# A two-layer convolution block on one core: the first statistics shared between two engines, parked products issued between them, two banks for the first running sums

## The chip, the core and the metric

The kernel runs on one core of a Trainium2 chip. The core has five engines that matter here, each with its own in-order list of instructions: PE (TensorE, matrix products), DVE (VectorE), ACT (ScalarE), POOL (GpSimd) and SP (SyncE, which here only issues DMAs). The metric is the device time of one execution in microseconds (us), as a median over runs.

## What is computed

The input x has 384 channels of 192x192 float32. Two layers follow each other; only the first matters for this change. Its shape, cut to the core:

```python
def _gn(v, G=32, eps=1e-5):                     # normalise over groups of 12 channels
    g = v.reshape(B_, G, C_ // G, H_, W_)
    m, s = jnp.mean(g, axis=(2, 3, 4)), jnp.var(g, axis=(2, 3, 4))
    return ((g - m) / jnp.sqrt(s + eps)).reshape(v.shape)

def layer0(x):                                  # x already normalised
    qkv = einsum('bchw,oc->bohw', x, w_qkv)     # 384 -> 1152 channels
    qkv = max over 2x2 pixels, then 3x3 depthwise convolution
    ...                                         # channel attention with top-k, gelu, projection

x = x + layer0(_gn(x))
x = x + conv7x7_depthwise(_gn(x))
```

Before any product of the first layer can be right, the mean and the variance of every group of 12 channels over all 36,864 pixels must be known, so all of x (56.6 MB) is read once for statistics alone.

## The kernel before

The 384 channels lie on three tiles of 128 partitions (`KT` = 3; the first two are `TWO`). The pixels are cut into 24 blocks (`NB`) of 8 image rows, 1536 pixels each (`BLK`). Statistics run over the blocks from 23 down to 0. The last three of them (2, 1, 0: `NX` = 3) stay in SBUF in the tiles `held`, because the products begin with them.

**First two tiles (lines 392 to 434).** SP loads one block of both tiles at a time (`xs`, 1536 KB) into a pool `xsp` of five buffers; a buffer can be loaded again when the engine that measured it is done. `summed` (335) measures a block on DVE, three `bn_stats` of 512 pixels for each tile. After block 3, `aggregate` (353) joins what has been measured into a mean and a variance per channel; three small products on PE (`total`, 339) make the group means `mids`, and `moments` (359) expresses the channel's moments about such a mean. The channels of the last group that tile two shares with tile three are measured apart (`xe`, 317). After block 0, `both` (367) adds the last three blocks, and `normed` (373) gives `rstd0`, with a power on POOL (382). ACT scales the rows of the weights `wq` of these two tiles by it (434).

**Parked products (436 to 470).** `begin(i)` multiplies one third of a held block by the weights of the first two channel tiles, and ACT copies the partial sum from its PSUM bank into SBUF (`spots`); the products of the third tile are added later. There are 24 such products. Twenty are copied away and the last four stay in their banks. Four banks (`bank_b0`, `bank_b1`, `bank_c`, `bank_d`) are used in turn, so a product needs the copy of the one four places before it. 21 of the products are issued in one loop (453) before the third tile's statistics, and three more after that tile's `most`.

**Third tile (457 to 482).** The same statistics for the third tile. From block 22 down to 4 two blocks are loaded at once (`xt`, 128x3072, six `bn_stats`), then block 3, then the held ones. After block 3 the group mean is made on PE (463), and at the end `both`, `total` and `normed` give the third tile's scale. Its weights are scaled on ACT (506), and `pooled` (665) adds the third tile's products (678) to the parked sums.

**After that (1014 to 1090).** In the loop over the blocks 0 and 1, DVE takes the 2x2 maximum (688) and runs the 3x3 depthwise sums of block 0 (`depthwise`, 719): nine steps for each of six channel tiles, the running sum in a PSUM bank. `sum_bank` (788) gives the bank: while block 0 is summed, the next of `bank_x`, `bank_y`, `bank_r` in turn. A finished sum is transposed by DVE (833) and squared by ACT (746). Then a loop over groups begins with `share`, `base` and `second` (1051 to 1066), whose products go to `bank_x` and `bank_y` and are copied by ACT (1055, 1061).

The order on an engine is what the framework's scheduler makes of the program; calls wrapped in `keep` stay in program order. The DMA queue of SP is in program order.

Of the kernel before, what the change touches and what calls it, by code (L numbers as in the profile page):

```python
# [8 lines left out]
F32 = mybir.dt.float32  # L9
AF = mybir.ActivationFunctionType  # L10
ALU = mybir.AluOpType
AX = mybir.AxisListType

P = 128
C = 384
KT = C // P
# [3 lines left out]
PS = HW // 2  # L20
# [6 lines left out]
NB = PS // PR  # L27
IR = 2 * PR
BLK = IR * HW
PB = PR * PS  # L30
SUB = BLK // 512
NX = 3
# [54 lines left out]
def conv_preact_d2(  # L87
# [17 lines left out]
    nc = tc.nc  # L105
# [153 lines left out]
    def load_x(b, name):  # L259
# [14 lines left out]
    bank_x, bank_y, bank_b0, bank_b1, bank_c, bank_d = [  # L274
        pb.tile([P, 512], F32, name=f"bank_{n}") for n in ("x", "y", "b0", "b1", "c", "d")
    ]
    pr = qx.enter_context(tc.tile_pool(name="pr", bufs=1, space=PSUM))
    bank_r = pr.tile([P, 512], F32, name="bank_r")

    def turns_of(banks):  # L280

        k = -1
        while True:
            k += 1
            yield banks[k % len(banks)]

    small = turns_of([bank_x, bank_y, bank_r])
# [10 lines left out]
    spots = [rowbuf[:, k * 512 : (k + 1) * 512] for k in range(3 * KT * ROW // 512)]  # L298
# [7 lines left out]
    TWO = KT - 1  # L306
    OVER = TWO * P // GC * GC + GC - TWO * P
    keep = tc.keep_in_program_order
    with tc.tile_pool(name="stp", bufs=1) as stp, tc.tile_pool(name="xsp", bufs=5) as xsp:
        st = stp.tile([P, KT, NB * SUB, 6], F32, name="st0")  # L310
# [21 lines left out]
        none = stp.tile([P, CT], F32, name="none")  # L332
        nc.gpsimd.memset(none, 0.0)

        def summed(kt, b, n, t):
            for j in range(n * SUB):
                nc.vector.bn_stats(st[:, kt, b * SUB + j, :], t[:, j * 512 : (j + 1) * 512])

        def total(name, n, terms):

# [9 lines left out]
        def sel(kt, jt):  # L350
            return gsel[:, kt, jt * P : (jt + 1) * P]

        def aggregate(kt, lo, hi, name):

            mv = stp.tile([P, 2], F32, name=f"mv0_{kt}_{name}")
            nc.vector.bn_aggr(mv, st[:, kt, lo * SUB : hi * SUB, :].rearrange("p n s -> p (n s)"))
            return mv

        def moments(mv, mid, name):

            d = stp.tile([P, 2], F32, name=f"ds0_{name}")
            nc.vector.tensor_tensor(d[:, 0:1], mv[:, 0:1], mid, ALU.subtract)
            nc.vector.tensor_tensor(d[:, 1:2], d[:, 0:1], d[:, 0:1], ALU.mult)
            nc.vector.tensor_tensor(d[:, 1:2], d[:, 1:2], mv[:, 1:2], ALU.add)
            return d

        def both(kt, most, mid):

            last = moments(aggregate(kt, 0, NX, "last"), mid, f"{kt}_last")
            nc.vector.scalar_tensor_tensor(most, last, NX / NB, most, ALU.mult, ALU.add)  # L370
            return most

# [14 lines left out]
        mids = stp.tile([P, KT + 1], F32, name="mids0")  # L387
        mve = stp.tile([P, 2], F32, name="mve")
        me = stp.tile([P, 1], F32, name="me")
        rest0 = (NB - NX) / NB  # L390
        most = [None] * KT
        for b in reversed(range(NB)):
            if b == NX - 1:
                most[:TWO] = [aggregate(kt, NX, NB, "most") for kt in range(TWO)]
                means = [mv[:, 0:1] for mv in most[:TWO]]
                terms = [
                    [(sel(0, 0), means[0]), (sel(1, 0), means[1])],
                    [(sel(0, 1), means[0]), (sel(1, 1), means[1]), (shared[:, 0:P], me)],
                    [(of, means[1]), (ones, me)],
                ]  # L400
                for k, i in ((0, 0), (1, 1), (KT, 2)):
                    ps = total(f"gs_mid0_{k}", 1, terms[i])
                    nc.vector.tensor_scalar_mul(mids[:, k : k + 1], ps, 1.0 / GC)
                de = moments(mve, mids[:, KT : KT + 1], "e")
                nc.vector.tensor_scalar_mul(de, de, 1.0 / EP)
                dm = [moments(most[kt], mids[:, kt : kt + 1], f"{kt}_most") for kt in range(TWO)]
                for d in dm:
                    nc.vector.tensor_scalar_mul(d, d, rest0)
            if b < NX:
                xb = held[b][:, 0:TWO]  # L410
            else:
                xb = xsp.tile([P, TWO, BLK], F32, name=f"xs{b}", tag="xs")
            nc.sync.dma_start(xb, xv[:, 0:TWO, b * BLK : (b + 1) * BLK])
            for kt in range(TWO):
                summed(kt, b, 1, xb[:, kt])
            if b == NB - 1:
                for j in range(EN // 384):
                    nc.vector.bn_stats(ste[:, j, :], xe[:, j * 384 : (j + 1) * 384])
                nc.vector.bn_aggr(mve, ste.rearrange("p n s -> p (n s)"))
                nc.vector.tensor_scalar_mul(me, mve[:, 0:1], 1.0 / EP)  # L420
        ds = [both(kt, dm[kt], mids[:, kt : kt + 1]) for kt in range(TWO)]
        terms = [
            [(sel(0, 0), ds[0]), (sel(1, 0), ds[1])],
# [12 lines left out]
        def begin(i):  # L436
            b, ct, g = begun_qk[i]
            ps = next(large)
            rows = held[b].rearrange("p t (r c) -> p t r c", c=HW)
            for kt in range(TWO):  # L440
                keep(
                    nc.tensor.matmul(
                        ps, wq[:, kt, ct * P : (ct + 1) * P], rows[:, kt, :, g * 64 : (g + 1) * 64],
                        start=(kt == 0), stop=(kt == TWO - 1), skip_group_check=True,
                    )
                )
            if i < len(spots):
                nc.scalar.copy(spots[i], ps)
                sums_qk[b, ct, g] = spots[i], False
            else:  # L450
                sums_qk[b, ct, g] = ps, True

        for i in range(len(spots) + 1):
            begin(i)


        kt = TWO
        mid = mids[:, kt : kt + 1]
        for b in [*range(NB - 2, NX, -2), NX, *reversed(range(NX))]:
            n = 2 if b > NX else 1  # L460
            if b == NX - 1:
                most = aggregate(kt, NX, NB, "most")
                ps = total(
                    "gs_mid0_2", 1,
                    [(sel(1, 2), means[1]), (shared[:, P:], me), (whole, most[:, 0:1])],
                )
                nc.vector.tensor_scalar_mul(mid, ps, 1.0 / GC)
                dm = moments(most, mid, "2_most")
                nc.vector.tensor_scalar_mul(dm, dm, rest0)
                for i in range(len(spots) + 1, len(begun_qk)):  # L470
                    begin(i)
            if b < NX:
                xb = held[b][:, kt]
            else:
                xb = xsp.tile([P, TWO, BLK], F32, name=f"xt{b}", tag="xs")
                xb = xb.rearrange("p k n -> p (k n)")[:, 0 : n * BLK]
            loaded = nc.sync.dma_start(xb, xv[:, kt, b * BLK : (b + n) * BLK]).ins
            summed(kt, b, n, xb)
        d = both(kt, dm, mid)
# [97 lines left out]
    with ExitStack() as bx:  # L577
# [141 lines left out]
        def depthwise(b, ct, dst, pin):  # L719

            r0 = b % 3 * PR
            acc = sum_bank(b)[:, 0:C].rearrange("p (r c) -> p r c", c=PS)
            for tap in range(9):
                i, j = divmod(tap, 3)
                src = ring[ct][:, r0 + i : r0 + i + PR, j : j + PS]
                w = wd[:, ct, tap : tap + 1]
                if tap == 0:
                    pin(
                        nc.vector.tensor_scalar(
                            acc, src, w, bdb[:, ct : ct + 1], ALU.mult, ALU.add  # L730
                        )
                    )
                else:
                    into = dst if tap == 8 else acc
                    pin(nc.vector.scalar_tensor_tensor(into, src, w, acc, ALU.mult, ALU.add))
                yield
# [48 lines left out]
        turning = {}  # L785
        sides = {}

        def sum_bank(b):

            if sum_pool is not None:  # L790
                return sum_pool.tile([P, C], F32, name=f"acc{b}", tag="tr")
            return next(small) if b == 0 else bank_r

        def pe_keep(ins):
            return keep(ins) if ins.ins.engine == mybir.EngineType.PE else ins
# [218 lines left out]
        last = None  # L1014
        for b in range(2):
            xb = held.pop(b)
            for ct in range(2 * KT):
# [13 lines left out]
                if last is not None:  # L1031
                    finish(*last)
                    last = None
                if b > 0:
                    last = b - 1, ct, dst, taps
# [55 lines left out]
        for n, (b, pair, half) in enumerate(groups):  # L1091
            s = n % 6
# [36 lines left out]
            if s in (4, 5) or (s == 0 and b > 2):  # L1129
                bb, p = (b, s - 4) if s else (b - 1, KT - 1)  # L1130
# [5 lines left out]
            first = early if scaling else early + 1 + (s < 4)  # L1136
# [249 lines left out]
    with tc.tile_pool(name="ap", bufs=1) as ap:  # L1386
# [8 lines left out]
        i = AHEAD - 1  # L1395
# [28 lines left out]
    for i in range(3):  # L1424
        t = sxp.tile([P, LEAD + CP * RB * RUN + LEAD], F32, name=f"sx{i}")
# [137 lines left out]
    for i in range(AHEAD, NBC):  # L1563
        j = i - 2
# [61 lines left out]
    with ExitStack() as ex_:  # L1626
# [255 lines left out]
        last = None  # L1882

        later = {2 * kt: kt for kt in range(1, KT)}
        for n in range(steps):
# [8 lines left out]
            apart = outp.tile([P, CP, 2, NT * NJ], F32, name=f"apart{n}", tag="apart", bufs=3)  # L1894
# [24 lines left out]
            for q in range(CP):  # L1919
                ps = sums(q, range(2 if q in ahead else 0, 3))  # L1920
                c = n * CB + 2 * q
# [24 lines left out]
            last = apart  # L1946
# [58 lines left out]
```

## Time and profile before

| | us |
|---|---|
| runs | 2703.38, 2695.53, 2695.43 |
| median | 2695.53 |
| profiled execution | 2711.91 |
| its span, first to last instruction | 2710.2 |

| engine | busy in the span, us |
|---|---|
| PE | 2512.9 |
| DVE | 2268.1 |
| ACT | 1419.6 |
| POOL | 1462.8 |

The profile is of one execution, whose time is some 16 us above the median; durations are of that execution. A line of a timeline gives the start, the duration, the engine, the source line, the operation, what it writes and reads with shapes, how often it is merged (x6), and in brackets how long the engine had been idle before it and what released it. A table of stretches gives, for each stretch, the busy time of the engines with the number of instructions, the granted TensorE clock, the busy share of the 16 DMA engines and the rate in GB/s. A product of a 128x512 operand shows as two passes, so a parked product over two channel tiles has four.

### The profile page before, as it was taken

The numbers are of one execution on the slowest core, as the hardware profiler recorded it, in microseconds if no ns is written. First come the engines' busy times: TensorE is split into PE (matmuls) and PEld (weight loads), VectorE is DVE, ScalarE is ACT, GpSimd is POOL, SyncE is SP. The second block draws the span as 40 slices with busy tenths as digits, with TensorE's granted clock in tenths as the row PEclk, the third lists the DMA queues.
The fourth block names the chain that finished last, engine by engine and source line by source line (L and its number), as shares of the span: only waits on it lengthen the run. The fifth ranks groups of instructions, "written<-read, shape, count | busy, mean of one in ns | idle before, by whom it ended". The sixth has DMA issues, their size and how long they took to land. (4 is left out here: it accounts for less than half of the span.)

```text
span 2710.2 us, 29562 instructions
## 1 busy us (share of the span) xinstructions
PE 2512.9 (93%) x8893; PEld 1632.4 (60%) x8893; DVE 2268.1 (84%) x3161; ACT 1419.6 (52%) x2710; POOL 1462.8 (54%) x1588
## 2 busy tenths in 40 slices
PE   0298999999999999999889989999999799999998
PEld 0144565656666656555556646666667577777776
DVE  7986788888888888888689969898888789888987
ACT  0032667676767676775112223223225577777776
POOL 1013788888887988875112311001001578787886
PEclk9999999999999999999999989999999899999999
DMA  9962354445453545433429996756747999999998
GB/s 378 394 245 53 117 163 135 137 139 165 131 169 102 175 128 170 128 98 76 136 80 331 372 316 210 250 195 221 239 143 246 331 347 367 371 372 367 372 368 263
DMA packets 467582, 609.59 MB, mean 225 GB/s; under 512 B 250160, under 2 KB 399264, under 8 KB 450656
## 3 DMA queue, kind: packets, MB, share of 16 engines
q1 hardware_dynamic: 406928, 311.80, 36.9%
q0 software_dynamic: 37376, 148.85, 15.4%
q10 hardware_dynamic: 23120, 147.07, 14.4%
q8 instruction: 71, 1.16, 0.2%
q14 instruction: 87, 0.71, 0.1%
HBM read 370.93 MB, written 208.21 MB: 214 GB/s over the span
## 5 line engine op out<-in xcount | busy, mean ns | idle before, releaser
L563 PE MATMUL pv<-xv,wq 128*128 128x384 f32 x1512 | 502.7, 493 | 27.2 <-DMA xv<-in_x_dram 13.5
L1909 PE MATMUL pc<-main,w 128*128 128x288 f32 x1536 | 435.2, 406 | 3.6 <-issue 2.2
L563 PEld LDWEIGHTS pv<-xv,wq 128*128 128x128 f32 x1512 | 290.8, 193 | 230.9 <-DVE rows L569 16.3
L1929 DVE TENSOR_SCALAR apart<-pc,rb 32x576 f32<-32x576 f32 x384 | 312.2, 813 | 75.9 <-PE pc L1909 51.8
L869 POOL TENSOR_TENSOR qk<-qk,more 128x384 f32<-128x384 f32 x290 | 309.6, 1074 | 110.2 <-ACT more L868 101.3
L1927 ACT ACTIVATE apart<-pc,rb 32x576 f32<-32x576 f32 x384 | 281.1, 732 | 133.2 <-PE pc L1909 128.4
L1543 POOL DMA_DIRECT2D sd<-sx x96 | 72.2, 755 | 507.4 <-DVE sx L1502 486.9
L1909 PEld LDWEIGHTS pc<-main,w 128*128 128x128 f32 x1536 | 289.8, 189 | 87.8 <-issue 3.2
L1375 DVE SCALAR_TENSOR_TENSOR vb<-rows,wd,vb 128x576 f32<-128x576 f32 x384 | 312.5, 816 | 10.8
L869 POOL TENSOR_TENSOR qk<-qk,rows 128x384 f32<-128x384 f32 x216 | 230.3, 1070 | 76.3 <-ACT rows L868 70.1
L1909 PE MATMUL pc<-aux,h 128*128 128x288 f32 x768 | 248.5, 406 | 0.5 <-issue 0.3
L901 DVE SCALAR_TENSOR_TENSOR bank_r<-ring,wd,bank_r 128x384 f32<-128x384 f32 x383 | 236.1, 617 | 6.9
L1868 POOL COPY res<-apart 128x1152 f32<-128x1152 f32 (+1 forms) x96 | 224.1, 2360 | 11.1 <-ACT apart L1927 7.3
L1009 PE MATMUL bank_b<-rows,more 128*128 128x384 f32 x528 | 220.4, 499 | 1.9 <-ACT bank_c L1111 0.9
L1502 DVE TENSOR_TENSOR sx<-xr,y 128x576 f32<-128x576 f32 x180 | 203.5, 1172 | 20.7 <-ACT y L1473 14.9
L569 DVE TENSOR_REDUCE rows<-pv 128x192 f32<-128x768 f32 x144 | 137.5, 955 | 69.7 <-PE pv L563 69.6
L1522 ACT ACTIVATE wq<-sx,negmid 128x1152 f32<-128x1152 f32 x96 | 120.6, 1256 | 114.5 <-DVE sx L1502 110.2
L1089 DVE TENSOR_TENSOR rows<-bank_c,rows 128x384 f32<-128x384 f32 x132 | 73.2, 555 | 127.3 <-PE bank_c L1009 69.0
L1752 DVE SCALAR_TENSOR_TENSOR w<-eye,sb,w 128x512 f32<-128x512 f32 x96 | 174.5, 1857 | 1.5
L1909 PEld LDWEIGHTS pc<-aux,h 128*128 128x128 f32 x768 | 144.9, 189 | 42.7 <-POOL main L1817 2.0
L868 ACT ACTIVATE more<-ring,wd 128x384 f32<-128x384 f32 x290 | 170.3, 608 | 0.0
L1009 PE MATMUL bank_x<-xq,wq 128*128 128x384 f32 x378 | 154.7, 491 | 1.0 <-ACT bank_b L1061 1.0
(342 smaller groups left out, 4803.9 us busy)
## 6 DMA issues: line engine op xcount, KB each, us to landing
sd<-sx POOLq DMA_DIRECT2D x96, 600.0 KB, 10.1
out_dram<-res SPq DMA_DIRECT2D x192, 288.0 KB, 10.7
main<-sd ACTq DMA_DIRECT2D x46, 1200.0 KB, 6.3
xr<-in_x_dram SPq DMA_DIRECT2D x45, 1152.0 KB, 12.8
xq<-in_x_dram SPq DMA_DIRECT2D x21, 2304.0 KB, 8.4
xv<-in_x_dram SPq DMA_DIRECT2D x126, 384.0 KB, 7.4
w<-wt ACTq DMA_DIRECT2D x46, 1024.0 KB, 7.5
xs<-in_x_dram SPq DMA_DIRECT2D x24, 1536.0 KB, 15.2
```

What stands on the lines that cost most here:

```text
L563: nc.tensor.matmul(ps[:, u, 0 : RB * HW], wq[:, kt, o : o + P], xb[:, u, kt, :], start=(kt == 0), stop=(kt == KT - 1),)
L868: keep(nc.scalar.mul(part.rearrange("p (h w) -> p h w", w=PS), src, w))
L869: keep(nc.gpsimd.tensor_tensor(flat, flat, part, ALU.add))
L901: nc.vector.scalar_tensor_tensor(into, src, w, before, ALU.mult, ALU.add)
L1009: nc.tensor.matmul(ps[:, 0:HN], lhs, rhs, start=start, stop=True, skip_group_check=True)
L1375: pin(nc.vector.scalar_tensor_tensor(dst, src, w, dst, ALU.mult, ALU.add))
L1502: nc.vector.tensor_tensor(bass.AP(flat.tensor, flat.offset + at(e) + a * RUN, [flat.ap[0], [JP, NT], [1, NJ], [at(f) - at(e), 2]],), xq[:, ...
L1752: nc.vector.scalar_tensor_tensor(mid, eye.unsqueeze(1).to_broadcast([P, 4, P]), sb[:, c : c + 1], mid, ALU.mult, ALU.add,)
L1868: keep(copy(res[ps, k], apart[ps, :, k].rearrange("p e n -> p n e")))
L1909: nc.tensor.matmul(ahead[q][:, k, 0 : NT * NJ], lhs, rhs, start=(j == 0), stop=(j == 2), skip_group_check=True,)
L1927: keep(nc.scalar.mul(dst, src, scale))
L1929: keep(nc.vector.tensor_scalar_mul(dst, src, scale))
```

## The change

The code of the statistics changes in three places.

1. Some blocks are measured on ACT and not on DVE. For the first two tiles these are the blocks 22, 18, 14, 10 and 6, for the third tile the pairs that begin at 18, 12 and 8. A first aggregate over block 23 (for the third tile, over the first pair) gives each channel a centre. ACT then adds the negative centre to the block in place (Identity) and squares it in place (Square), and takes the sum over the pixels of each into `powers`. `rest_of` turns these sums into a mean and a variance and joins them with those that DVE measured.
2. The loop of 21 parked products is taken apart: three are issued ahead of the third tile's first load, and two ahead of each further load of a pair.
3. `sum_bank` gives `bank_r` and `bank_y` in turn for block 0.

```diff
         def summed(kt, b, n, t):
+            if b in apart[kt]:
+                k = apart[kt].index(b)
+                if k == 0:
+                    first = stp.tile([P, 2], F32, name=f"first{kt}")
+                    got = st[:, kt, NX * SUB : NX * SUB + SUB, :]
+                    nc.vector.bn_aggr(first, got.rearrange("p n s -> p (n s)"))
+                    nc.vector.tensor_scalar_mul(centre[:, kt : kt + 1], first[:, 0:1], -1.0)
+                for i, (func, bias) in enumerate(
+                    ((AF.Identity, centre[:, kt : kt + 1]), (AF.Square, 0.0))
+                ):
+                    nc.scalar.activation(
+                        t, t, func, bias=bias, accum_out=powers[:, kt, k, i : i + 1]
+                    )
+                return
             for j in range(n * SUB):
-                nc.vector.bn_stats(st[:, kt, b * SUB + j, :], t[:, j * 512 : (j + 1) * 512])
+                slot = b * SUB + j if b < NX else taken[kt]
+                taken[kt] += int(b >= NX)
+                nc.vector.bn_stats(st[:, kt, slot, :], t[:, j * 512 : (j + 1) * 512])
...
+        def rest_of(kt, most, mid):
+            d = moments(most, mid, f"{kt}_most")
+            here = (NB - NX - blocks_apart[kt]) / NB
+            nc.vector.tensor_scalar_mul(d, d, here)
+            n = len(apart[kt])
+            mv = stp.tile([P, 2], F32, name=f"mv0_{kt}_apart")
+            nc.vector.tensor_reduce(
+                mv, powers[:, kt, 0:n].rearrange("p n s -> p s n"), AX.X, ALU.add
+            )
+            nc.vector.tensor_scalar_mul(mv, mv, 1.0 / (blocks_apart[kt] * BLK))
+            sq = stp.tile([P, 1], F32, name=f"sq0_{kt}")
+            nc.vector.tensor_tensor(sq, mv[:, 0:1], mv[:, 0:1], ALU.mult)
+            nc.vector.tensor_tensor(mv[:, 1:2], mv[:, 1:2], sq, ALU.subtract)
+            nc.vector.tensor_tensor(mv[:, 0:1], mv[:, 0:1], centre[:, kt : kt + 1], ALU.subtract)
+            other = moments(mv, mid, f"{kt}_apart")
+            nc.vector.scalar_tensor_tensor(
+                d, other, blocks_apart[kt] / NB, d, ALU.mult, ALU.add
+            )
+            return d
...
-        for i in range(len(spots) + 1):
-            begin(i)
+        began = 0
...
-        for b in [*range(NB - 2, NX, -2), NX, *reversed(range(NX))]:
+        for at, b in enumerate([*range(NB - 2, NX, -2), NX, *reversed(range(NX))]):
             n = 2 if b > NX else 1
+            upto = min(2 * at + 3, len(spots) + 1) if b >= NX else len(spots) + 1
+            for i in range(began, upto):
+                begin(i)
+            began = upto
             if b == NX - 1:
-                most = aggregate(kt, NX, NB, "most")
+                most = aggregate(kt, NX * SUB, taken[kt], "most")
...
-                dm = moments(most, mid, "2_most")
-                nc.vector.tensor_scalar_mul(dm, dm, rest0)
+                dm = rest_of(kt, most, mid)
...
-        def sum_bank(b):
+        def sum_bank(b, ct=0):
             if sum_pool is not None:
                 return sum_pool.tile([P, C], F32, name=f"acc{b}", tag="tr")
-            return next(small) if b == 0 else bank_r
+            return (bank_r, bank_y)[ct % 2] if b == 0 else bank_r
```

What the scheduler makes of it, in the order of instructions of the changed program (cut; the line numbers are those of the changed kernel). On ACT, around the third tile's last pair that it measures:

```
L488 TensorCopy more<-bank_b 128x512          the copy of the 17th parked product
L352 Activation xt,powers<-xt,centre 128x3072   Identity of block pair 8
L488 TensorCopy more<-bank_b 128x512          the copy of the 18th
L352 Activation xt,powers<-xt 128x3072          Square of block pair 8
L488 TensorCopy more<-bank_c 128x512
```

On DVE, in the same stage:

```
L359 BNStats st<-xt 128x6 x6                  block pair 6
L388 TensorReduce mv_2_apart<-powers 128x2    needs ACT's last Square
L391, L393, L394, L395                        small operations on its result
L359 BNStats st<-xt 128x6 x6                  block pair 4
L359 BNStats st<-xt 128x6 x3                  block 3
L359 BNStats st<-xs 128x6
L378 BNStatsAggregate mv_2_most<-st 128x2
```

In the first two tiles the reduction of tile one's sums stands behind block 7's statistics and ahead of block 5's. The orders of PE, POOL and SP are those of before.

## What was predicted, ahead of the run

> **What bounds the kernel now.** The page gives PE 93% of the span, but its slices show PE idle in the first two of forty: the first 120 us are statistics of x, and from about 122 us PE is busy almost without a break. So what the change is worth is read from when PE gets its first real work, and from when the normalised weights of the third channel tile let `pooled` begin (line 678). I read the table of stretches first, then the timelines of DVE, ACT and PE up to 240 us, then the waits.
>
> Table of stretches (PE, PEld, DVE, ACT, POOL busy; granted clock; DMA share; GB/s):
>
> ```profile
> 40.00:80.00 40.00, 0.00 (x0) 0.00 (x0) 38.60 (x64) 0.00 (x0) 0.00 (x0) 1.00 1.02 416
> 80.00:100.00 20.00, 0.00 (x0) 0.00 (x0) 19.48 (x32) 0.00 (x0) 0.00 (x0) 1.00 1.02 416
> 100.00:120.00 20.00, 5.55 (x24) 5.35 (x24) 15.50 (x50) 0.00 (x0) 0.00 (x0) 1.00 1.02 425
> ```
>
> DVE and the DMA engines are both full there, and ACT is empty. Which of the two sets the pace? Timeline of DVE:
>
> ```profile
> 30.26 68.00 DVE L337 BATCH_NORM_STATS2 st<-xs 128x6 f32<-128x512 f32 x108 [0.28 <-DMA xs<-in_x_dram]
> 98.18 3.57 DVE L356 BATCH_NORM_AGGREGATE mv_most<-st 128x2 f32<-128x378 f32 x2
> ...
> 105.53 10.76 DVE L337 BATCH_NORM_STATS2 st<-xs 128x6 f32<-128x512 f32 x18
> 116.22 0.63 DVE L356 BATCH_NORM_AGGREGATE mv_last<-st 128x2 f32<-128x54 f32 x2
> ```
>
> The load of block 3 is issued at 79.35 and lands 15.2 us later, at 94.55; DVE begins block 3 at 98.18 - 3.6 = 94.6. Each block is measured as it lands, one every 3.78 us (68.00 / 18). The last three loads, which wait for no buffer, land 18.6, 21.8 and 25.1 us after issues at 79.8, 80.3 and 80.8: 3.75 us apart. So DMA sets the pace, and DVE, at 18 instructions in 10.76 us (0.598 each, 3.59 a block), only just keeps up. Freeing DVE here brings no earlier block.
>
> Third tile and what follows, timelines of all engines, then of PE and ACT:
>
> ```profile
> 120.38 37.47 DVE L337 BATCH_NORM_STATS2 st<-xt 128x6 f32<-128x512 f32 x63
> ...
> 122.02 6.11 PE L442 MATMUL bank_b<-xs,wq 128*128 128x512 f32 x8 [2.17 <-ACT wq L434]
> ...
> 158.36 1.84 DVE L356 BATCH_NORM_AGGREGATE mv_most<-st 128x2 f32<-128x378 f32 x1
> ...
> 160.58 0.28 PE L344 MATMUL bank_r<-mv_most,gsel 128*128 128x1 f32 x2
> ```
> ```profile
> 167.20 0.38 PE L344 MATMUL bank_x<-ds_most,whole 128*128 128x2 f32 x2 [0.30 <-DVE ds_most L370]
> ...
> 170.35 2.86 PE L678 MATMUL bank_b<-xs,wq 128*128 128x512 f32 x4
> ...
> 232.64 1.54 PE L1009 MATMUL bank_x<-rows,more 128*128 128x384 f32 x2 [3.33 <-DVE qk L735]
> 237.12 1.65 PE L1009 MATMUL bank_x<-xs,wq 128*128 128x384 f32 x2 [2.94 <-ACT rows L1055]
> ```
> ```profile
> 236.09 0.52 ACT L746 ACTIVATE qk<-qk 128x384 f32<-128x384 f32 x1 [1.94 <-DVE turns L833]
> 236.52 0.19 ACT L746 ACTIVATION_READ_ACCUMULATOR qk<-qk 128x1 f32 x1
> 236.61 0.46 ACT L1055 COPY rows<-bank_x 128x384 f32<-128x384 f32 x1
> ```
>
> Two chains meet here within a microsecond. PE's parked products run 122.02 to 166.3: two in 5.95 us, then 22 at 1.716. DVE's statistics end just before PE asks for them, both at 160.58 (`mv_most`) and at 167.20 (`ds_most`, a wait of 0.30).
>
> **What the Trainium skill says.** "ScalarE: Activation LUTs", section "What ACT_TABLE_LOAD costs": an ACTIVATE with a pointer bias takes about 280 ns + 0.833 ns per element, with immediates 186 ns. The trace agrees: 128x1152 with a bias took 1256 ns (1240 by the rule), 128x384 without one 520 (506). "TensorE: Matmul & The Clock Gate", section "What's actually happening": after an idle window of about 3.4 us the array runs at half rate until it has been busy as long. The trace agrees roughly: passes at 122 us are 0.85 us apart for 5 us, then 0.43. "DMA: Bandwidth & Descriptors", section "Where 436 GB/s comes from", puts a ceiling of 435 GB/s on the ports; 416 to 425 here is near it.
>
> **The change part by part.** In the changed program's order of instructions PE, POOL and SP stand as before (the parked products are only written at another place in the source); DVE and ACT differ. Each engine runs its own order, so a wait holds up all behind it. SP's list of loads is the same, but a load into a buffer that ACT measured now waits for ACT.
>
> *First two tiles.* Blocks 22, 18, 14, 10, 6 leave DVE: 30 instructions x 0.598 = 17.9 us less. On ACT each costs two Identity (estimate from the rule: 1.56, with the accumulator read 1.58) and two Square (1.49) = 6.1 us, beside 15 us between such blocks, so ACT keeps up; the buffer is held 6.1 instead of 3.6 us, with three loads still in flight. The loads stay at 3.78. But the last ACT block is 6, and DVE, in its order of instructions, reads ACT's sums after block 7 and before block 5. Block 6 lands at 94.55 - 3 x 3.78 = 83.2; ACT runs Identity, Identity, Square and has the first sum at 83.2 + 4.65 = 87.85. DVE, done with block 7 near 83.1, waits, reduces (0.2) and is at 88.1. Block 5: 91.7. Nine small operations: +0.9. Blocks 4 and 3: 99.8 (98.2 before). The two aggregates shrink from 378 to 288 numbers, 2.8 us against 3.57: 102.6. Means over PE as before, 2.95: 105.5. Fifteen small operations for twelve: +1.05, 106.6. Eighteen statistics with six more small ones between: 10.76 + 0.45, 117.8 against 116.2. The rest is the same, so PE starts at 123.65 instead of 122.02: **+1.6**. If the ACT sums are in time, -0.5; if every small operation with a wait costs 0.2, +3.
>
> *Third tile.* DVE loses 18 instructions, 10.7 us; ACT gains three pairs of 3072 elements (Identity 2.84, Square 2.75), placed between copies of parked products. In program order the pair of block 8 comes after the 17th product: on ACT the order is copy 17, Identity, copy 18, Square. Product 17 ends at 123.65 + 5.95 + 15 x 1.716 = 155.35, its copy at 155.95, Identity at 158.8, copy 18 at 159.4, Square with its read at 162.25. Its load isn't late: it waits for ACT's Square of block 18 (about 140.5), and lands 6 us later. PE's banks come free in time: product 21 ends at 162.2. On DVE the reduction of ACT's sums stands before blocks 4, 3 and 2. Block 6 has landed by 150.4 (two loads behind 140.5) and is measured at 154.0; DVE then **waits 8.3 us**. From 162.3: reduction and four operations 0.95, blocks 4 and 3 nine x 0.595 = 5.4, one of block 2 0.6, aggregate of 270 numbers 1.37: `mv_most` at 170.6, where it was at 160.2. Behind it, in PE's order, stand three more parked products, so PE idles from 162.2 to 170.65 and goes cold: tiny products 0.6, six passes at 0.85, six at 0.43, end 179.0. DVE's tail took 7.0 us (160.2 to 167.2); with five more small operations 7.35: 177.9. So PE is last by a microsecond. Three small products 0.7: 179.8 against 167.58, and line 678 follows 2.8 us later in both: 182.5 against 170.35. **+12.2, the 1.6 included.** Without the cold array 178.3: +10.8. With 0.2 us for each waiting small operation: +14.
>
> *Two banks for the first running sums.* `share(0)` no longer waits 3.33 us for bank_x. But its copy (line 1055) stands on ACT behind the square of the last qk, which waits for DVE's last transpose; it starts at 236.61 as before, and `base` needs that copy. DVE executes in order and has as many operations. **0**; bound: `pooled`'s last products end at 229.3; if the share (1.5) and its copy (0.5, and gaps of 0.4) followed at once, 237.1 would become 231.7 and 5.4 us be won.
>
> Everything later is paced from line 678, loads and POOL's weights too, so the shift reaches the end: span 2710.2 + 12.2 = 2722.4, its execution 2711.9 + 12.2 = 2724.1. The median, 16 us under that execution, moves as much: 2695.5 + 12.2 = 2707.7.
>
> **Rivals.**
> 1. The wait for ACT's sums costs nothing. Place: the reduction before block 4; it decides if the Square of block 8 is over before 154.0. Then PE's products run through, end at 167.95, and line 678 begins at 171.4: +1.1, 2696.6, not slower. For it: ACT is idle half the time here. Against: copy 17 can't start before 155.35.
> 2. The bank change pays 5.4: +6.8, 2702.3. Against: ACT's order.
> 3. DMA is paced by DVE after all. Third-tile loads ran at 3.56 us a block; 21 x 0.22 = 4.6 us earlier, and with 1 a change of -3.5 (2692), with 2 also -8.9 (2686.6). Against: 3.75 us for loads that waited for nothing.
> 4. ACT holding five buffers 2.5 us longer starves the loads: up to +12 more, 2719. Against: three loads, 11 us of work, in flight.
>
> **How the numbers follow.** Forecast 0.70 (its own range 2704 to 2711, from the bounds of the two waits and the array's rate); rivals 0.12, 0.08, 0.04, 0.06. 0.3% is 8.1 us, about what a measurement of this kernel can tell from no change. Slower takes nearly all of the forecast and rival 4, and part of rival 2: 0.76; faster only the far end of 3 and what isn't foreseen: 0.05; the rest 0.19. The range leaves out rivals 1, 3 and the far end of 4.
>
> **What would show it.** Right: loads still 3.78 us apart; DVE waiting on ACT's `powers` for 4 to 5 us near 83 and about 8 near 154; PE waiting about 8 us for `mv_most`, then slow passes; line 678 near 182; the copy of line 1055 still behind line 746. Wrong: line 678 at or before 172, no DVE wait on ACT in the third tile, or the copy of line 1055 ahead of the square.

## The result, and the profile after

| | runs | median, us | range, us |
|---|---|---|---|
| before | 8 | 2696.19 | 2694.96 to 2703.38 |
| changed | 8 | 2707.18 | 2702.71 to 2723.69 |

The ratio is 1.0044, 95% interval 1.0027 to 1.0061: the changed kernel is slower by 11.0 us. The forecast was 2707.7, 12.2 us over before.

The profiled execution of the changed kernel took 2707.93 us (span 2706.2), less than the profiled one of before (2711.91). These two totals mustn't be set against each other. Marks that stand in both traces show why:

| mark | before, us | changed, us | shift |
|---|---|---|---|
| first parked product (line 442, now 482) | 122.02 | 121.93 | -0.1 |
| TensorE asks for `mv_most` and has it (344, now 366) | 160.94 | 168.88 | +7.9 |
| first product of the third tile (678, now 719) | 170.35 | 180.82 | +10.5 |
| ACT's copy of the first shared sums (1055, now 1096) | 236.61 | 247.09 | +10.5 |
| first instruction of a line in the second half (ACT, 1522, now 1563) | 1420.0 | 1430.5 | +10.5 |
| last instruction of that line | 2119.3 | 2116.9 | -2.4 |

From 170 to 1420 us the shift is constant. Then 13 us vanish in a stretch in which no instruction was changed. The table of stretches for that part, before and then changed (columns: window, length, busy time of PE, PEld, DVE, ACT, POOL, then granted clock, DMA share and GB/s):

```profile
1420.00:2119.00 699.00, 666.82 (x2279) 435.68 (x2277) 609.46 (x693) 213.13 (x464) 109.61 (x147) 0.97 0.75 253
```
```profile
1430.50:2117.00 686.50, 663.51 (x2279) 432.98 (x2277) 609.80 (x697) 213.35 (x465) 109.94 (x147) 0.99 0.75 258
```

The stretch with the same 2279 products took 12.5 us less, and the granted clock in it is 0.99 in the execution of the changed kernel and 0.97 in the other. That belongs to the executions, not to the change: in a second pair of traces, both from one chip (under "Both kernels again"), the first and the last instruction of the same line come at 1420.5 and 2123.5 us before and at 1429.6 and 2136.4 in the changed kernel, so the shift is +9.1 there and grows to +12.9. So what follows is read from the marks, and the medians say what a run costs.

**First two tiles.** Timeline of DVE, changed kernel (start, duration, engine, line, operation, what it writes and reads, count, and in brackets the idle time before it and its releaser):

```profile
70.70 11.10 DVE L359 BATCH_NORM_STATS2 st<-xs 128x6 f32<-128x512 f32 x18 [3.68 <-DMA xs<-in_x_dram]
86.72 0.16 DVE L388 TENSOR_REDUCE mv_apart<-powers 128x2 f32<-128x10 f32 x1 [4.92 <-ACT xs L352]
...
91.23 7.21 DVE L359 BATCH_NORM_STATS2 st<-xs 128x6 f32<-128x512 f32 x12
98.35 2.75 DVE L378 BATCH_NORM_AGGREGATE mv_most<-st 128x2 f32<-128x288 f32 x2
```

The wait for ACT's sums of block 6 is there, 4.92 us. Yet the aggregates begin at 98.35, where they began at 98.18 before: the wait ends earlier than forecast (86.7 instead of 87.85), since the blocks landed faster. The table of stretches of the changed kernel shows it; before, the same stretch had 416 in its last column:

```profile
80.00:100.00 20.00, 0.07 (x1) 0.10 (x1) 15.05 (x34) 6.16 (x8) 0.00 (x0) 1.00 1.02 426
```

**Third tile.** Timelines of ACT, of DVE and of PE, changed kernel:

```profile
154.49 2.86 ACT L352 ACTIVATE xt<-xt,centre 128x3072 f32<-128x3072 f32 x1
...
157.34 0.57 ACT L488 COPY more<-bank_b 128x512 f32<-128x512 f32 x1
157.80 2.77 ACT L352 ACTIVATE xt<-xt 128x3072 f32<-128x3072 f32 x1
```
```profile
148.56 3.66 DVE L359 BATCH_NORM_STATS2 st<-xt 128x6 f32<-128x512 f32 x6 [9.11 <-DMA xt<-in_x_dram]
160.70 0.16 DVE L388 TENSOR_REDUCE mv_apart<-powers 128x2 f32<-128x6 f32 x1 [8.48 <-ACT xt L352]
161.43 5.43 DVE L359 BATCH_NORM_STATS2 st<-xt 128x6 f32<-128x512 f32 x9
167.38 1.35 DVE L378 BATCH_NORM_AGGREGATE mv_most<-st 128x2 f32<-128x270 f32 x1
```
```profile
168.88 0.56 PE L366 MATMUL bank_r<-mv_most,whole 128*128 128x1 f32 x2 [7.71 <-DVE mv_most L378]
169.30 3.76 PE L482 MATMUL bank_b<-xs,wq 128*128 128x512 f32 x4
172.85 2.93 PE L482 MATMUL bank_c<-xs,wq 128*128 128x512 f32 x4
175.62 1.88 PE L482 MATMUL bank_d<-xs,wq 128*128 128x512 f32 x4
...
180.82 2.83 PE L719 MATMUL bank_b<-xs,wq 128*128 128x512 f32 x4
...
208.72 5.31 PE L719 MATMUL bank_b<-xs,wq 128*128 128x512 f32 x12
```

Read from the top, this is the whole loss. ACT's Square of block pair 8 ends at 160.57. DVE's reduction, queued ahead of the blocks 4, 3 and 2, waited 8.48 us for it, though none of those blocks needs it. PE waited 7.71 us for `mv_most` with three parked products queued behind, and when they came, the first two took 3.76 and 2.93 us in place of 1.96 and 1.88.

**Banks.** Timelines of PE and of ACT, changed kernel, and the group of twelve passes in the kernel before that answers to the one at 208.72:

```profile
239.62 0.81 PE L1050 MATMUL bank_x<-rows,more 128*128 128x384 f32 x2
247.61 1.65 PE L1050 MATMUL bank_x<-xs,wq 128*128 128x384 f32 x2 [7.18 <-ACT rows L1096]
```
```profile
247.09 0.46 ACT L1096 COPY rows<-bank_x 128x384 f32<-128x384 f32 x1
```
```profile
198.25 5.31 PE L678 MATMUL bank_b<-xs,wq 128*128 128x512 f32 x12
```

The wait of 3.33 us ahead of the first shared product is gone, and the wait behind it grew from 2.94 to 7.18: ACT's copy stands 66.27 us behind the first product of the third tile, as before (66.26), and 38.37 us behind the first group of twelve passes (38.36 before).

### The profile page after: what moved, and what is told of

Its sections match the earlier page's. It is cut to its first block, busy times and chain, and to the rows that moved or that the text cites. A ratio compares the mean times of both kernels' runs of the same rounds, so it can differ in the third digit from the quotient of the medians.

```text
span 2706.2 us, 29605 instructions
## 1 busy us (share of the span) xinstructions
PE 2510.6 (93%) x8893; PEld 1629.4 (60%) x8893; DVE 2234.7 (83%) x3146; ACT 1466.9 (54%) x2762; POOL 1467.6 (54%) x1588
## 5 line engine op out<-in xcount | busy, mean ns | idle before, releaser
L1793 DVE SCALAR_TENSOR_TENSOR w<-eye,sb,w 128x512 f32<-128x512 f32 x96 | 165.8, 1765 | 1.5
```

The costliest lines, as they stand in the source:

```text
L1793: nc.vector.scalar_tensor_tensor(mid, eye.unsqueeze(1).to_broadcast([P, 4, P]), sb[:, c : c + 1], mid, ALU.mult, ALU.add,)
```

## The experiments

They ran on four chips. On three of them the kernel before takes 2720 us, on the one of the last row 2710; each is compared with runs of the kernel before on its own chip. "Start" is the first parked product, "tile 3" the first product of the third tile, both from the profiled execution. TensorE runs the first parked products at half rate for a time that differs from execution to execution (the eight passes of the first two took 5.30 to 6.66 us). So a "late distance" is given too: from the third parked product, which lies behind that phase, to the first group of twelve passes of the third tile. It was 70.28 us in the first trace of the kernel before (127.97 to 198.25) and 80.66 in that of the changed one (128.06 to 208.72).

| run | time, us | before there | ratio, 95% interval | start | tile 3 | distance | late distance |
|---|---|---|---|---|---|---|---|
| before, again | 2715.30 (one run) | 2720.40 | | 121.99 | 170.57 | 48.58 | 70.28 |
| changed, again | 2729.57 | 2720.40 | 1.0034 [1.0021, 1.0048] | 121.66 | 179.93 | 58.27 | 80.46 |
| third tile on DVE | 2721.22 | 2720.79 | 1.0001 [0.9992, 1.0009] | 122.97 | 171.41 | 48.44 | 70.28 |
| reduction late | 2720.23 | 2720.79 | 0.9997 [0.9989, 1.0006] | 121.94 | 170.44 | 48.50 | 72.52 |
| products in one loop | 2731.45 (one run) | 2720.79 | | 122.09 | 180.82 | 58.73 | 80.78 |
| first tiles on DVE | 2728.81 (one run) | 2720.79 | | 120.36 | 179.45 | 59.09 | 80.73 |
| changed, idle products | 2718.26 (one run) | 2719.81 | | 121.45 | 178.19 | 56.74 | 80.05 |
| banks alone | 2715.25 (one run) | 2719.81 | | 121.96 | 170.84 | 48.88 | 68.63 |
| block 2 on ACT too | 2718.16 | 2719.81 | 0.9992 [0.9982, 1.0002] | 119.82 | 167.57 | 47.75 | 70.51 |
| the same, idle products | 2717.80 | 2719.81 | 0.9988 [0.9979, 0.9997] | 121.15 | 168.78 | 47.63 | 70.28 |
| the same, again | 2718.14 | 2720.40 | 0.9991 [0.9981, 1.0001] | 121.09 | 168.64 | 47.55 | 70.30 |
| block 2 on ACT, buffers aligned | 2706.95 | 2710.15 | 0.9989 [0.9981, 0.9996] | 118.25 | 166.66 | 48.41 | 70.28 |

Single runs of one kernel lie up to 18 us apart here, so what is read from a single run rests on the last four columns.

**Third tile back on DVE.** The sharing of the first two tiles, the split loop and the banks stay.

```diff
-        apart = [(22, 18, 14, 10, 6)] * TWO + [(18, 12, 8)]
-        blocks_apart = [5] * TWO + [6]
+        apart = [(22, 18, 14, 10, 6)] * TWO + [()]
+        blocks_apart = [5] * TWO + [0]
```

> The third tile's statistics are all on DVE again, the first two tiles stay shared, the rest is the changed kernel. My theory (DVE waits 8 us in its own order for ACT's last Square, and the parked products behind it on PE wait for DVE): no wait of DVE on ACT in the third tile, mv_most ready near 160, no 7.7 us wait of PE, the line of the third tile's first product (170.35 before, 180.82 in the changed kernel) at 170 to 171, and the whole time back to that of the kernel before, 2696 within 3. Rival (the products issued between the statistics, or the two banks, cost the time): the line stays near 180 and the time near 2707.

The distance falls to 48.44, within 0.2 us of the kernel before, the late distance to 70.28, that of before, and the time is that of before within 0.1%. So the loss lies in the sharing of the third tile. What is left, a start 1.0 us later than before (122.97 against 121.99), is the price of sharing the first two.

**The reduction alone put later.** The changed kernel, with ACT measuring its blocks of the third tile as before; only the reduction of its sums is issued behind DVE's aggregate and not ahead of block 4.

```diff
+            late = tc.issue_after(joint[kt]) if kt == TWO else ExitStack()
+            with late:
-            nc.vector.tensor_reduce(
+              nc.vector.tensor_reduce(
                 mv, powers[:, kt, 0:n].rearrange("p n s -> p s n"), AX.X, ALU.add
             )
```

> Only the place of one instruction changes: DVE reduces ACT's sums of the third tile after it has joined its own (mv_most), not before it measures the blocks 4, 3 and 2. My theory (the place in the queue is most of the loss, the rest is loads that wait for buffers that ACT holds): mv_most at about 161 to 163 instead of 168.7, the first product of the third tile at 172 to 174 instead of 180.82, the time 2698 to 2700, 7 to 9 us under the changed kernel. Rival (ACT is too late in any place, because the final moments need its sums too, or the loads are too late): still near 179 to 181, 2705 or more.

Tile 3 begins at 170.44, 10.4 us ahead of the changed kernel and earlier than the 172 to 174 expected. Timelines of DVE and of PE of this kernel:

```profile
147.69 3.66 DVE L360 BATCH_NORM_STATS2 st<-xt 128x6 f32<-128x512 f32 x6 [8.42 <-DMA xt<-in_x_dram]
152.49 5.44 DVE L360 BATCH_NORM_STATS2 st<-xt 128x6 f32<-128x512 f32 x9 [1.15 <-DMA xt<-in_x_dram]
...
158.44 1.35 DVE L379 BATCH_NORM_AGGREGATE mv_most<-st 128x2 f32<-128x270 f32 x1
159.72 0.16 DVE L393 TENSOR_REDUCE mv_apart<-powers 128x2 f32<-128x6 f32 x1
```
```profile
166.87 0.38 PE L367 MATMUL bank_x<-ds_most,whole 128*128 128x2 f32 x2 [0.86 <-DVE ds_most L418]
...
170.44 3.76 PE L724 MATMUL bank_b<-xs,wq 128*128 128x512 f32 x4
...
199.59 5.31 PE L724 MATMUL bank_b<-xs,wq 128*128 128x512 f32 x12
```

No wait for ACT is left, and the distance is 48.50, that of before. The sharing of the third tile gains nothing all the same. DVE has 18 statistics fewer, some 10.7 us, but its waits for loads, 8.42 and 1.15 us, take most of that, and at the end PE still waits for DVE's `ds_most` (0.86 us, 0.30 before).

Nor is quite all of the loss gone in this trace. Its start had a short half-rate phase, which flatters the distance; the late distance is 72.52, 8 us under the changed kernel and 2.2 over the kernel before. These 2.2 us are the longer wait for `ds_most` (0.56), slower small products behind it (3.24 us against 2.82) and more passes at half rate in tile 3 (1.25). Whether they come from the place of the reduction or from chance, one trace doesn't tell; the time shows no loss.

**All parked products in one loop again.** The changed kernel with the loop of 21 undivided (`upto = len(spots) + 1`).

> The 21 parked products are written in one loop ahead of the third tile's statistics again, as in the kernel before; the sharing stays. The order on ACT moves by a single copy (the copy of the 19th product comes ahead of the last Square). My theory: the last Square ends 1.7 us later, the wait of DVE grows from 8.5 to about 10 us, the first product of the third tile is at 182 to 183 instead of 180.8. Rival (issuing the products between the statistics is itself the loss): the line comes back to 170 to 173.

Tile 3 begins at 180.82, to the digit as in the changed kernel and below the expected band. ACT's order did move by a copy, but its last Square ends 38.86 us behind the start (38.64 in the changed kernel), 0.2 us later and not 1.7, and DVE waits 8.90 us for it (8.48). The late distance is 80.78. So the split loop moves next to nothing.

**First two tiles back on DVE.** The third tile stays shared.

```diff
-        apart = [(22, 18, 14, 10, 6)] * TWO + [(18, 12, 8)]
-        blocks_apart = [5] * TWO + [6]
+        apart = [()] * TWO + [(18, 12, 8)]
+        blocks_apart = [0] * TWO + [6]
```

> The first two tiles are measured on DVE alone again, the third tile stays shared. My theory (sharing the first two tiles is worth nothing, since the loads set the pace and DVE loses at block 6 what it gained): PE's parked products begin within 0.5 us of the changed kernel's 121.9, blocks 3.78 us apart again instead of 3.7, and the first product of the third tile is at 180 to 182. Rival (sharing the first two tiles is a gain that hides part of the loss): products begin 2 us or more later, and the line at 183 or more.

The loss of the third tile stays whole: distance 59.09, late distance 80.73. But the start was a miss. It came at 120.36, 1.6 us ahead of the kernel before (121.99), though DVE measured these two tiles with the same instructions. Table of stretches of this kernel:

```profile
80.00:100.00 20.00, 0.56 (x2) 0.50 (x2) 19.84 (x30) 0.00 (x0) 0.00 (x0) 1.00 1.02 426
```

Something other than the sharing gave the loads 426 GB/s in place of 416. Against this start, the changed kernel's sharing of the first tiles costs 1.3 to 1.6 us (121.66 and 121.93).

**The bank choice alone.** The kernel before with only the new `sum_bank`.

```diff
-            return next(small) if b == 0 else bank_r
+            return (bank_r, bank_y)[ct % 2] if b == 0 else bank_r
```

> The kernel before with only the bank choice of the change. My theory (the copy of the first shared product stands on ACT behind the square of the last qk): the first shared product runs on PE 3 us earlier, but its copy starts within 0.3 us of where it did (236.6 in the kernel before, and the same distance, 66.3, from the first product of the third tile), so nothing is gained. Rival: the copy starts 3 to 5 us earlier and the time falls by as much.

Timelines of PE and of ACT of this kernel:

```profile
197.09 5.31 PE L678 MATMUL bank_b<-xs,wq 128*128 128x512 f32 x12
...
227.99 0.81 PE L1009 MATMUL bank_x<-rows,more 128*128 128x384 f32 x2
235.97 1.65 PE L1009 MATMUL bank_x<-xs,wq 128*128 128x384 f32 x2 [7.17 <-ACT rows L1055]
```
```profile
235.46 0.46 ACT L1055 COPY rows<-bank_x 128x384 f32<-128x384 f32 x1
```

The share is issued at once and PE then waits 7.17 us for ACT's copy. The copy stands 64.62 us behind tile 3's first product, 1.64 less than before, where 0.3 had been allowed. That isn't the banks: the first two rows of tile 3 took 1.96 and 1.02 us in this execution and 2.86 and 1.86 in the one of before, so 1.74 us fewer went to half-rate passes there (the first parked products, 6.66 us against 6.11, had spent 0.55 more). From the first group of twelve passes, which lies behind those rows, to the copy it is 38.37 us here and 38.36 in the kernel before. The banks didn't move the copy.

**Idle products to keep the array busy.** Eight products that nothing reads, put ahead of the group mean of the third tile in the changed kernel; they fill PE's wait.

```diff
+                for _ in range(8):
+                    keep(nc.tensor.matmul(bank_x, ident, held[0][:, 0, 0:512], start=True, stop=True))
                 ps = total(
                     "gs_mid0_2", 1,
```

> The changed kernel with eight idle products on PE where it waits for mv_most. My theory (the wait lets the array go cold, and this puts PE behind DVE by a microsecond or two): the last three parked products take 5.2 to 5.6 us instead of 8, and the first product of the third tile comes 1.5 to 2 us earlier, at 178.8 to 179.3 where the changed kernel had 180.82. Rival (the cold array is hidden behind DVE): the line stays within 0.4.

Timeline of PE of this kernel:

```profile
159.23 7.03 PE L506 MATMUL bank_x<-xs,ident 128*128 128x512 f32 x16
...
167.66 1.96 PE L482 MATMUL bank_b<-xs,wq 128*128 128x512 f32 x4
169.46 1.88 PE L482 MATMUL bank_c<-xs,wq 128*128 128x512 f32 x4
171.17 1.88 PE L482 MATMUL bank_d<-xs,wq 128*128 128x512 f32 x4
```

The three parked products take 5.72 us in place of 8.57, 2.85 less. Tile 3's distance falls only by 1.5 to 2.2 us (56.74 against 58.27 and 58.89), for DVE's `ds_most` is late next, and the 24 small products behind it took 3.88 us where they had taken 2.82. Part of that is the start's half-rate phase, which was 0.5 to 1.0 us shorter here (5.33 us for eight passes, 5.87 and 6.28 in the changed kernel's traces). Without it 1.0 to 1.2 us are left at tile 3, and in the late distance 0.4 to 0.6 (80.05 against 80.46 and 80.66). So the cold array is about a microsecond of the 10.5 at most, and the wait itself the rest.

**A better split.** Since the loads pace the first two tiles, what counts there is DVE's work after the last load. This version gives ACT block 2 of the first two tiles as well, leaves the third tile to DVE, and issues the reduction behind the group means. ACT writes its values of the held block 2 to a scratch area, since the block is used later.

```diff
-        apart = [(22, 18, 14, 10, 6)] * TWO + [(18, 12, 8)]
-        blocks_apart = [5] * TWO + [6]
+        apart = [(22, 18, 14, 10, 6, 2)] * TWO + [()]
+        blocks_apart = [6] * TWO + [0]
+        ends = [2] * TWO + [NX]
...
+            with tc.issue_after(behind):
+                nc.vector.tensor_reduce(
```

> The third tile is on DVE alone; in the first two tiles ACT measures block 2 as well, into a spare buffer and not in place since the products need it, and DVE reduces ACT's sums only after the group means. My theory (sharing pays only where it takes work out of the stretch after the last loads, and only with the reduction behind everything that must not wait): no wait of DVE on ACT near 83, parked products begin at 118 to 118.5 (122 in the changed kernel, 120.4 with the first tiles on DVE alone), the first product of the third tile at 166 to 167.5, and 2 to 4 us less than the kernel before. Rival (the loads set this end too, or the added small operations eat it): products begin at 120 or later and the time does not differ.

The start moves to 119.82, 2.2 us ahead of before but short of the 118 to 118.5 expected, and tile 3 by 3.0 (0.8 of it by a shorter half-rate phase). In the time it is 1.6 us, and the interval holds 1, so the gain of 2 to 4 us is not shown.

**The same with nine idle products**, seven of them ahead of the last group sums and two behind:

> As the kernel with block 2 on ACT, and seven idle products on PE between the group means and the final sums, two more ahead of the first parked product, which keep the array busy and write nothing that is read. My theory (a cold array costs the first parked products 2.5 us and the small sums ahead of them about 1): the first two parked products take 3.4 to 4 us instead of 6; but the third tile's statistics on DVE end last then, so the first product of the third tile moves by 1 to 1.5 us only, 165 to 166. Rival (the array's rate isn't set by what PE did before): the first two still take 6 us and the line stays.

The idle products gave nothing at the start: it came at 121.15, 1.3 us later than without them, because DVE's order now had a block of the third tile (3.65 us) ahead of the normalisation, and the first two rows of parked products still took 5.40 us (5.35 without), where 3.4 to 4 had been expected. The time was 0.9988 of before. Timed again:

> The version with blocks 2, 6, 10, 14, 18 and 22 of the first two tiles on ScalarE, the third tile on VectorE alone and the idle products, timed again. Theory: the earlier start is worth 1 to 3 us, ratio 0.9988 to 0.9997 as before. Rival (the earlier result was chance): interval holds 1 with its middle above 0.9997.

0.9991, and the interval now just holds 1. Taken together this version is ahead of before by about 2 us, at the edge of what can be measured.

**Both kernels again, on a chip of the experiments.**

> The kernel before, unchanged, profiled on the chip of the experiments, so that their traces have a partner from the same chip. Theory (all of the shift comes in the third tile's wait): the parked products begin between 121.0 and 123.5 us depending on the pace of the loads, no wait of TensorE for mv_most, and line 678 stands 48 to 49 us behind the start of the parked products. Rival (the bank choice or the loop split moves something as well): that distance differs from the one of the kernels without the wait by more than 1 us.

> The changed kernel, unchanged, timed on the chip of the experiments. Theory: 10 to 12 us over before, ratio 1.0037 to 1.0045, and line 719 some 58 to 60 us behind the start of the parked products (before plus 10 to 11). Rival (part of the first comparison's +11 us was the chip or the execution): ratio under 1.002.

The before kernel repeats its marks: start 121.99 (122.02 in the first trace) and 415 to 418 GB/s. The changed kernel repeats too: 425 GB/s, distance 9.7 us longer than before's, time 9.2 us longer, a ratio of 1.0034, a little under the 1.0037 expected. So the two rates of the loads belong to the programs, not to the executions or the chips.

**Where the load buffers lie.** The addresses in the built programs sort the kernels. The change puts new small tables ahead of the load buffers and so moves them. The remainder is that of the buffers' byte address in a partition, divided by 256; all five buffers of a kernel share it:

| kernels | remainder | GB/s, 40 to 100 us |
|---|---|---|
| before (twice), banks alone | 224 | 415 to 418 |
| block 2 on ACT (three times) | 160 | 416 to 418 |
| third tile on DVE | 128 | 417 to 418 |
| changed (twice), reduction late, products in one loop, first tiles on DVE, changed with idle products | 0 | 424 to 426 |

All kernels of the last row also share the third tile with ACT, so one run had to part the two (the expectation below calls "block 2 on ACT" e5):

```diff
-        powers = stp.tile([P, KT, 6, 2], F32, name="powers")
+        powers = stp.tile([P, KT, 10, 2], F32, name="powers")
```

> The version of e5 (block 2 of the first two tiles on ScalarE too, third tile on VectorE alone, no idle products) with a table of sums four columns longer. None of them is used; they move the load buffers behind the table by 96 bytes, from 164000 to 164096, a multiple of 256 bytes per partition. Theory (the loads' pace comes from where the buffers lie: 425 GB/s in all kernels whose buffers stand on such multiples, 415 to 418 in the others): 424 to 426 GB/s from 40 to 100 us, parked products begin near 118.1 instead of 119.8, line 727 near 165.9 instead of 167.6, 1.7 us less than e5, ratio about 0.9986. Rival (the pace comes from the third tile's work on ScalarE, which all kernels with 425 GB/s so far had): 417 GB/s and 119.8 as in e5, ratio 0.9992.

Tables of stretches, first without and then with the 96 bytes:

```profile
80.00:100.00 20.00, 0.56 (x2) 0.50 (x2) 15.93 (x25) 8.20 (x11) 0.00 (x0) 1.00 1.01 417
```
```profile
80.00:100.00 20.00, 1.48 (x7) 1.46 (x7) 15.29 (x24) 9.76 (x13) 0.00 (x0) 1.00 1.01 425
```

The rate went to 425 and the start from 119.82 to 118.25, and this kernel shares no block of the third tile: the place of the buffers sets the rate. The chip of this run has no other trace; on each of the other three chips traces of both rates stand side by side, sorted by the address. Tile 3 came 0.9 us earlier, not 1.7, as the first two rows of parked products took 6.19 us instead of 5.35. The time is 0.9989 of before, interval 0.9981 to 0.9996: this version is ahead of the kernel before by 3 us, and so of the changed one (1.0034 and 1.0044), but its lead over the one without the 96 bytes (0.9992) is too small for these runs.

## Why the prediction was right

The forecast (+12.2 us; measured +11.0 by the medians) held, with its main mechanism. By its steps:

- **What bounds the stage.** Right: the loads pace the first two tiles, and freeing DVE brought no earlier block. DVE now waits 3.68 us for a load in front of 18 of its instructions.
- **First two tiles, +1.6.** The part that it worked out is right. The wait for block 6's sums is 4.92 us (4.75 by its figures, 83.1 to 87.85), and sharing costs 1.0 us between buffers off a multiple of 256 bytes and 1.3 to 1.6 us between aligned ones. What failed is the step "The loads stay at 3.78". They came every 3.71 us (ACT's first Identity of block 14 began at 52.36 and that of block 6 at 82.00, both released by the load: 29.64 / 8), 2% faster, and took back the 1.6: the start moved by -0.1. That the two cancel was chance. The cause was on none of the lists of what the change moves, since only addresses moved. Rival 3 had the loads faster for another reason, DVE's pace; "first tiles on DVE" has 425 GB/s with DVE as loaded as before, so that rival falls. The 3.56 us a block on which it built is how far apart DVE freed buffers in the third tile (loads issued at 124.06 and 127.62), with the loads at 389 GB/s from 130 to 150 us; it isn't a rate that loads had reached.
- **Third tile, +10.6 beside that.** Right, in its parts too. Counted from the first parked product, against the forecast:

| | forecast, us | measured, us |
|---|---|---|
| Square of pair 8 ends | 38.6 | 38.64 |
| DVE's wait for it | 8.3 | 8.48 |
| `mv_most` done | 46.95 | 46.80 |
| last parked product ends | 55.35 | 55.57 |
| first product of tile 3 | 58.85 | 58.89 |

  "Reduction late" shows that the order of one reduction on DVE makes all of it at this mark, and 8 of 10.2 to 10.4 us in the late distance.
- **The cold array, 1.4 of it.** Somewhat less: in "changed, idle products" it is 1.0 to 1.2 at tile 3, the start's half-rate phase taken off, and 0.4 to 0.6 in the late distance.
- **Two banks, 0.** Right: ACT's copy didn't move, in the changed kernel nor alone. The bound of 5.4 didn't come into play.
- **Everything later is paced from line 678.** Right as far as 1420 us, where the shift was still 10.5. Behind that the executions differ by more than the change does (-2.4 in one pair of traces, +12.9 in the other), so the end is read from the medians.
- **Rival 1** (the wait costs nothing) would have come true with the reduction behind the aggregate. **Rival 4** (ACT starves the loads) didn't show in the first two tiles: the loads were faster. DVE's 9.11 us wait for a pair in the third tile is the load that the forecast had held up by ACT: it let DVE begin at 26.63 us behind the start, 26.75 by its figures. It costs nothing since the wait for the Square follows it.

The sum was 1.2 us too high against the medians. The first tiles' term alone was 1.7 too high; that the medians lie 0.5 us above the 10.5 of the marks is within the spread of the changed kernel's runs, 2702.7 to 2723.7. On the chip of the second pair of traces the change cost 9.2 us, and tile 3 came 9.4 us later.

## What to carry to other kernels

An engine that is given work so that another is relieved returns its result through the other's in-order queue: look where the first instruction that reads it stands, and put it behind all work that doesn't need it. Moving that one reduction was worth 8 to 10 us here, while the relief that it belonged to gained nothing. When a change adds or removes small buffers, compare the addresses of the large load buffers too, for they may move, and the loads' rate with them.

## What the hardware showed unexpectedly

- From 40 to 100 us, loads of 128 partitions by runs of 6144 bytes went at 424 to 426 GB/s into buffers on a multiple of 256 bytes and at 415 to 418 off it. The Trainium skill, "DMA: Bandwidth & Descriptors", section "How a descriptor splits into AXI transactions", states that a transaction starts at a multiple of 256 bytes and that what it covers ahead of the descriptor still costs beats. An estimate from that page: a run of 6144 bytes takes 192 beats if aligned, 199 at remainder 224, 197 at 160 and 196 at 128, so 2.1 to 3.6% more. Measured: 425 against 416 at 224 (2.2%) and against 417 at 160 and 128 (1.9%), less than the estimate and with the lowest rate at 224, as the page has it. The page words it for what a transaction reads, while here the address written to was moved. That the split is the cause is not shown; the runs show the dependence on the address.
- The half-rate phase of TensorE at the same place, after nearly the same idle time, lasted differently from execution to execution: the first eight passes took 5.30 to 6.66 us in the starts above, where eight at full rate take 3.60. "TensorE: Matmul & The Clock Gate", section "What's actually happening", lets the rate change with windows that run freely, which fits. It moved marks by up to 1.4 us at the start and should be taken off before two marks are compared.
- Nine idle products in front of the parked ones didn't shorten that phase (5.40 us); 2.89 us of idle time still followed them. Eight of them with 0.84 us of idle time behind did, 5.72 against 8.57 us for three products. That the idle time in between makes the difference is a reading of two cases, not tested alone.
